# Attention and a depthwise convolution on one core: another order of the first loads and statistics, and q and k projected in pairs ahead of the scores

## The chip, the cores and the metric

The program runs on one core of a Trainium2 chip. The metric is the device time of one execution in microseconds, the median of several. The core has five engines that run their own instruction queues side by side and wait for each other by semaphores: TensorE (PE, matrix products), VectorE (DVE, elementwise work and statistics), ScalarE (ACT, activations and copies), GpSimd (POOL) and SyncE (SP). Transfers are issued from the queues of SyncE, GpSimd and, at the end, ScalarE.

## The reference

Input x has 16 images of 384 channels and 32 by 32 pixels, so 1024 positions. Everything is float32. Two layers follow each other, each added to its input:

```python
# layer 0
g = group_norm(x)                      # 32 groups of 12 channels, over group and positions
q, k, v = g @ w_qkv.T                  # 8 heads of 48 channels
a = softmax(q @ k.T * 48 ** -0.5)      # 1024 x 1024 for each head and image
x = x + (a @ v) @ w_proj.T + b_proj
# layer 1
w = mean of the four 90-degree rotations of the 7 x 7 filters
x = x + depthwise_conv_7x7(group_norm(x), w, pad=3)
```

## The kernel before

**Tiling.** Channels lie on partitions, in three blocks of 128 (`NK = 3`); positions lie along the free dimension. Heads are worked in pairs, a pair being a unit, so an image has four units. A unit is done in two halves of 512 query positions, and a half is a group of eight steps. A step makes the scores of 128 keys against 512 queries for both heads (`s_step`, TensorE, line 472, into one of three PSUM buffers), ScalarE exponentiates them (line 480, into one of eight buffers), and `av_step` (line 488) multiplies them with v and accumulates. TensorE thus alternates: eight score steps, eight steps with v, and so on, 64 of each in an image. After each half ScalarE copies the accumulator out (`take`, line 499).

**Between the groups** TensorE has other work: q and k of the next image (`qk_step`, line 421, twelve 512-column matmul instructions each, copied from PSUM by ScalarE at line 428; q and k of one of three channel blocks are a pair), v at the start of an image (`v_step`, line 447), and the projection of the image before (`proj_step`, line 541). The first and the last image are projected at once, in parts (`proj_part`, line 579).

**The softmax sums** come out of the product with v as an extra row. They go through DRAM to be spread over partitions, are inverted (`invert`, line 513) and multiplied in (`divide`, line 524) on VectorE.

**Group norm of x.** Image 0 has its statistics from VectorE (line 239) and the averages over groups from TensorE with masks (`groups_on_pe`, line 307). Image 1's go through DRAM (`x_channels`, `gather`, `groups`, `spread`). Images 2 to 15 are read a first time for their statistics alone, as 42 pieces of 512 KB (`stream_in` on GpSimd's queue, `stream_stats` on VectorE, line 361, through six buffers). Once all are in, one gather (`stream_gather`), one evaluation (`stream_groups`) and one spread (lines 404 and 410) give the scale and shift of all of them, `x_sc`. When an image is loaded for its projection (`load_x`, line 155, into the one x buffer, once v of the image before has been projected), ScalarE normalises it in place (`x_apply`, line 338, three activations).

**Group norm of the sum x1.** For most images the mean comes from ScalarE's accumulators (`x1_means`, line 943), the squares from three more activations (`x1_squares`, line 270), and scale and shift from ScalarE's Ln and Exp (`x1_groups`, lines 288 to 290, with two table loads) and a spread through DRAM (lines 259 and 263). Then three activations make the normalised xn (`x1_chains`, line 338, output `xn`). For the images in `ON_VECTOR` VectorE makes the statistics instead.

**The convolution** is 49 multiply-and-adds ("taps") for each image and channel block on VectorE (line 607), up to three blocks taken in turn. For the last two images some blocks are done on TensorE instead, as products with diagonal matrices (line 712), added by VectorE (line 727). The last block of all is summed in two halves that line 867 adds. Stores to `out` go from GpSimd's queue (line 620).

**Order.** Nothing is scheduled at run time. The Python program keeps two clocks, `clock` for TensorE and `vclock` for VectorE, and writes each engine's instructions in the order of a planned time. `after(wait, cost, f)` puts work for VectorE (and GpSimd's transfers) at a due time; `catch_up(clock)` writes due work, and taps in what is left. `applies` is the queue of ScalarE's normalisations with due time and cost; `act_slot(free)` writes those that are due and fit into `free` us. `chunks` holds the pairs of q and k to be issued, and `other` decides, twice in a group (after the scores and after the products with v), whether a projection or a piece of `chunks` goes in there. `ready[b]` is the planned time from which image b is normalised. Before, a counter of credit, 0.45 more at each call, let two chunks through when it had reached 2, in whichever of the two places that was:

```python
def other(done):
    credit = min(credit + 0.45, 2.0)
    ...
    elif credit >= 2:
        while chunks and credit >= 1:
            ...
            if kind == "qk" and i % 2 == 0:
                act_slot(4.5)
            issue(chunks.popleft())
            credit -= 1
```

At the end the program checks that no softmax sum is out of range (`check_vector`, `check_tensor`), and would otherwise run a slower general version (`run(True)`), which never happens with these inputs.

Of the kernel before, what the change touches and what calls it, by code (L numbers as in the profile page):

```python
# [44 lines left out]
def kernel(  # L45
# [47 lines left out]
    again = consts.tile([1, 1], I32, name="again")  # L93
    wsym = consts.tile([P, NK, KS, KS], F32, name="wsym")


    with tc.tile_pool(name="wcpool", bufs=1) as wcpool:
        wc = wcpool.tile([P, NK, KS, KS], F32, name="wc")
        nc.gpsimd.dma_start(
            wc.rearrange("p k i j -> p k (i j)"),  # L100
            w_conv.rearrange("(k p) o i j -> p k (o i j)", p=P),
        )
        w90 = wcpool.tile([P, NK, KS, KS], F32, name="w90")
        nc.vector.tensor_tensor(
            w90, wc, wc[:, :, :, ::-1].rearrange("p k a b -> p k b a"), ALU.add
        )
        nc.vector.tensor_tensor(wc, w90, w90[:, :, ::-1, ::-1], ALU.add)
        nc.vector.tensor_scalar(wsym, wc, 0.25, None, ALU.mult)

    def run(general):  # L110
        tag = "g" if general else "f"
        with ExitStack() as stack:
# [37 lines left out]

            def load_x(b):
                xns[b] = xpool.tile([P, NK, N], F32, tag="x", name=f"x_{b}")
                queue = nc.gpsimd if b else nc.sync
                for k in range(NK):
                    queue.dma_start(  # L155
                        xns[b][:, k, :], x[b, k * P : (k + 1) * P].rearrange("p h w -> p (h w)")
                    )
# [662 lines left out]
            def after(wait, cost, f):  # L820

                nonlocal count
                count += 1
                heapq.heappush(later, (now() + wait, count, cost, f))
# [83 lines left out]
            lims = []  # L908

            applies, pending = deque(), []  # L910
            ON_VECTOR = (B - 3, B - 2)

            def project(b):
                nonlocal clock
# [47 lines left out]

            def x1_groups(b, st):
                st.groups_x1()
                applies.append((clock + 8.0, 3.7, lambda: x1_chains(b, st)))

            def act_slot(free):

# [77 lines left out]
            late["masks"] = masks_0.rearrange("p (b c) -> p b c", c=P)  # L1046
            st.groups_on_pe(late["masks"])
            for k in range(NK):
                engine = (nc.vector, nc.gpsimd, None)[k]
                st.apply(xns[0][:, k, :], xns[0][:, k, :], k, engine)  # L1050
            ready[0] = 0.0
            queue(0)
            every = [(b, k) for b in range(2, B) for k in range(NK)]
            for n, bk in enumerate(every):
                after(4.0 * n, 0.0, lambda bk=bk: stream_in(*bk))
                after(4.0 * n + 10.0, 1.3, lambda bk=bk: stream_stats(*bk))
            after(4.0 * len(every) + 14.0, 0.0, stream_gather)
            after(4.0 * len(every) + 34.0, 3.6, stream_groups)

            def check_vector():  # L1060

                lim = small.tile([P, 2], F32, tag="lim", name="lim")
                every = sums.rearrange("p u c -> p (u c)")
                nc.vector.tensor_reduce(lim[:, 0:1], every, AX.X, ALU.max)
                nc.vector.tensor_reduce(lim[:, 1:2], every, AX.X, ALU.min)
                nc.vector.tensor_scalar(lim[:, 0:1], lim[:, 0:1], SUM_HIGH, None, ALU.is_le)
                nc.vector.tensor_scalar(lim[:, 1:2], lim[:, 1:2], SUM_LOW, None, ALU.is_ge)
                ones = small.tile([P, 1], F32, tag="ones", name="ones")
                nc.vector.memset(ones, 1.0)
                lims.append((ones, lim))  # L1070
# [27 lines left out]
                if (h, part) == (1, 1):  # L1098
                    after(6.0, 1.2, lambda: conv_on_pe_end(b, k))

            def other(done):

                nonlocal credit
                credit = min(credit + 0.45, 2.0)
                catch_up(clock)
                if proj and proj[0][0] <= clock:
                    project(proj.popleft()[1])
                elif credit >= 2:
                    while chunks and credit >= 1:
                        kind, cb, i = chunks[0]  # L1110
                        first = {"qk": 2 * NT * (i // 2), "rest": 2 * NT * 3}[kind]
                        if ready.get(cb, 1e9) > clock or done < first:
                            break
                        if kind == "qk" and i % 2 == 0:
                            act_slot(4.5)
                        issue(chunks.popleft())
                        credit -= 1
                catch_up(clock)

            def fast_finish(b):  # L1120
# [24 lines left out]
                    return True  # L1145
                return False

            credit = 0.0
            for b, n0, size in [
                (b, b * PER_B + sum(SIZES[:g]), SIZES[g]) for b in range(B) for g in range(len(SIZES))  # L1150
            ]:
                r = n0 - b * PER_B
                if n0 == NS - PER_B:
                    last_image = clock
                if r == 0:
                    while chunks:
                        issue(chunks.popleft())
                    if b + 1 < B:
                        queue(b + 1)
                for n in range(n0, n0 + size):  # L1160
                    s_step(n)
                clock += (size * US_STEP + US_TURN) / 2
                if r == 0 and b - 1 == FAST[0]:
                    fast_end(b - 1)
                if r == 0:
                    for i in range(NT // 2):
                        issue(("v", b, i))
                ending = b in FAST and r + size == PER_B
                if ending:
                    catch_up(clock)  # L1170
                    divide_at_once(NP * b + NP - 1, 0)
                    vclock += 4.2
                    for o in range(NK):
                        proj_part(b, o, (0, 1))
                    clock += 2 * US_PROJ
                else:
                    if r and pending and b - 1 in FAST:
                        applies.append((clock, 3.7, pending.pop()))
                    catch_up(clock)
                    act_slot(4.5)  # L1180
                    other(r + size)
                for n in range(n0, n0 + size):
                    av_step(n)
                    u, h, i = n // (2 * NT), n // NT % 2, n % NT
                    if i == NT - 1:
                        take(u, h)
                clock += (size * US_STEP + US_TURN) / 2
                if n0 // (2 * NT) < (n0 + size) // (2 * NT):
                    finish((n0 + size) // (2 * NT) - 1)
                if ending:  # L1190
                    catch_up(clock)
                    assert not invs and not waiting
                    fast_finish(b)
                else:
                    other(r + size)
                if b == 1 and r == 0:
                    conv_prepare()
                    nc.sync.dma_start(wp, w_packed)
                if b == B - 1:

                    if once("mat_0", r >= 16):
                        mat = flat2(xpool.tile([P, NK, N], F32, tag="x", name="mat_0"))
                        conv_matrices(0, mat)
                        late["w3"] = mat[:, 2 * SH * KS * CH :][:, 0:C]
                    if once("w", r >= 32 and b - 1 in x1_stats):
                        nc.sync.dma_start(wp, w4[:, 0:NK])
                        nc.sync.dma_start(late["w3"], w4[:, NK])
                    if once("mat_1", r >= 24):
# [12 lines left out]
                if b == B - 1 and r in (32, 40, 48):  # L1221
                    loads(1)
# [3 lines left out]
            fast_end(B - 1)  # L1226
            clock += 7.0
            vclock = clock
            after(4.0, 2.6, check_vector)
            while later or chains or active or pe_conv:  # L1230
                if pe_conv:
                    if pe_conv[0][0] == B - 1 and lims:
# [53 lines left out]
```

## Time and profile before

| | us |
|---|---|
| time, median of 3 (2974.22 to 2976.72) | 2974.3 |
| span of the profiled execution | 2976.5 |
| TensorE busy | 2926.9 (98%) |
| VectorE busy | 2580.1 (87%) |
| ScalarE busy | 1414.6 (48%) |
| GpSimd busy | 198.7 (7%) |

In the profile a line such as `L421 PE MATMUL ps_qk<-x,wqk` names the source line, the engine, the operation, and what it writes and reads. In the timeline the first two numbers are the start and the length of a run of like instructions in us, `x24` is how many they are, and the bracket says how long the engine had been idle before and who released it. Many numbers overlap, since the engines run side by side; idle time counts only where it is TensorE's, or whatever engine sets the end.

### The profile page before, as it was taken

How to read it: one execution, taken by the hardware profiler on the slowest of the kernel's cores; microseconds unless marked ns; L12 is line 12 of the kernel's file. 1: busy time of each engine (PE TensorE's matmuls, PEld its weight loads, DVE VectorE, ACT ScalarE, POOL GpSimd, SP SyncE). 2: the span in 40 equal slices, each digit the busy share in tenths (PEclk: the TensorE clock that was granted, in tenths of full speed). 3: DMA queues.
4: the chain of work that ended last, by engine and by line, in shares of the span. 5: the costliest groups of instructions: out<-in, count | busy, mean ns of one | idle time of the engine just before them, and what ended most of it. 6: DMA issues, size and time to landing. Idle time of an engine off the chain costs nothing.

```text
span 2976.5 us, 30347 instructions
## 1 busy us (share of the span) xinstructions
PE 2926.9 (98%) x11590; PEld 1185.5 (40%) x11590; DVE 2580.1 (87%) x2596; ACT 1414.6 (48%) x1683; POOL 198.7 (7%) x307
## 2 busy tenths in 40 slices
PE   7999899999999999999999999999999999999997
PEld 4334343343434434343343434334343433434333
DVE  0535990999989999899998999899998999999998
ACT  2432445445464544645545464555436464444610
POOL 0311201000000100000000000000000000000000
PEclk9999999999999999999999999999999999999999
DMA  2741112031311203121121312202131220312324
GB/s 74 254 116 41 24 31 72 15 67 37 69 34 33 68 24 66 37 62 41 26 70 30 66 37 56 47 22 60 44 66 37 46 57 15 67 37 52 108 57 115
DMA packets 72460, 169.72 MB, mean 57 GB/s; under 512 B 30080, under 2 KB 32496, under 8 KB 70768
## 3 DMA queue, kind: packets, MB, share of 16 engines
q0 software_dynamic: 29760, 97.67, 12.1%
q1 hardware_dynamic: 40784, 66.40, 9.8%
q10 hardware_dynamic: 1760, 3.61, 0.5%
q8 instruction: 93, 1.52, 0.2%
q14 instruction: 63, 0.52, 0.1%
HBM read 120.18 MB, written 29.35 MB: 50 GB/s over the span
## 4 chain that ended last, share of the span: by engine, by line


## 5 line engine op out<-in xcount | busy, mean ns | idle before, releaser
L607 DVE SCALAR_TENSOR_TENSOR x<-xn,wsym,x 128x899 f32<-128x899 f32 (+11 forms) x2181 | 2351.0, 1149 | 29.7 <-ACT xn L338 29.7
L480 ACT ACTIVATE e<-ps_s 128x1024 f32<-128x1024 f32 x1024 | 952.4, 1051 | 54.6 <-PE ps_s L472 51.4
L472 PE MATMUL ps_s<-qk 48*128 48x512 f32 x4096 | 914.2, 596 | 0.0
L488 PE MATMUL acc<-e,v 128*64 128x512 f32 x4096 | 907.2, 595 | 0.0
L472 PEld LDWEIGHTS ps_s<-qk 48*128 48x128 f32 x4096 | 376.8, 185 | 533.7 <-ACT e L480 257.2
L421 PE MATMUL ps_qk<-x,wqk 128*128 128x512 f32 x1152 | 512.6, 602 | 18.1 <-ACT x L338 15.8
L488 PEld LDWEIGHTS acc<-e,v 128*64 128x64 f32 x4096 | 283.2, 137 | 607.9 <-issue 601.7
L499 ACT COPY o<-acc 128x512 f32<-128x512 f32 x128 | 75.2, 587 | 644.9 <-PE acc L488 644.9
L421 PEld LDWEIGHTS ps_qk<-x,wqk 128*128 128x128 f32 x1152 | 217.5, 192 | 310.8 <-issue 275.8
L428 ACT COPY qk<-ps_qk 128x1024 f32<-128x1024 f32 x96 | 97.2, 1012 | 384.1 <-PE ps_qk L421 384.1
L447 PE MATMUL ps_v<-wv,x 128*128 128x384 f32 x768 | 254.7, 492 | 0.0
L541 PE MATMUL ps_proj<-o,wp 128*128 128x512 f32 x504 | 218.6, 592 | 0.0
L447 PEld LDWEIGHTS ps_v<-wv,x 128*128 128x128 f32 x768 | 146.0, 192 | 110.3 <-ACT e L480 11.4
L524 DVE TENSOR_TENSOR o<-o,inv 128x1024 f32<-128x1024 f32 x62 | 75.4, 1217 | 132.1 <-DMA inv<-inv 110.9
L456 ACT COPY v<-ps_v 128x384 f32<-128x384 f32 x128 | 55.1, 483 | 187.1 <-PE ps_v L447 187.1
L541 PEld LDWEIGHTS ps_proj<-o,wp 128*128 128x128 f32 x504 | 95.8, 190 | 117.6 <-issue 111.9
L155 POOL DMA_DIRECT2D x<-in_x x45 | 24.1, 543 | 1503.8 <-PE ps_v L447 1308.1
L361 DVE BATCH_NORM_STATS2 bs_all<-xs 128x6 f32<-128x512 f32 x84 | 52.1, 679 | 82.7 <-DMA xs<-in_x 82.7
L549 ACT ACTIVATE x<-ps_proj,bp 128x1024 f32<-128x1024 f32 x42 | 46.8, 1115 | 126.4 <-PE ps_proj L541 126.4
L712 PE MATMUL ps_conv<-sh,mat 128*32 128x464 f32 (+3 forms) x784 | 83.9, 584 | 0.0
L338 ACT ACTIVATE xn<-x,sc_x 128x1024 f32<-128x1024 f32 x44 | 52.1, 1284 | 28.6 <-DVE sc_x L328 28.5
L338 ACT ACTIVATE x<-x,x_sc 128x1024 f32<-128x1024 f32 x42 | 48.9, 1229 | 17.4 <-DMA x_sc<-gr_all 17.4
(110 smaller groups left out, 536.5 us busy)
## 6 DMA issues: line engine op xcount, KB each, us to landing
x<-in_x POOLq DMA_DIRECT2D x93, 512.0 KB, 5.4
inv<-inv SPq DMA_DIRECT2D x124, 256.0 KB
out<-x POOLq DMA_DIRECT2D x48, 512.0 KB, 3.6
xs<-in_x POOLq DMA_DIRECT2D x42, 512.0 KB, 6.0
qk<-qk SPq DMA_DIRECT2D x96, 128.0 KB
sh<-xd SPq DMA_DIRECT2D x34, 160.0 KB
o<-o SPq DMA_DIRECT2D x84, 64.0 KB
sh<-xd ACTq DMA_DIRECT2D x22, 160.0 KB
```

Source lines behind the costliest of these rows:

```text
L338: nc.scalar.activation(dst, src, AF.Identity, bias=self.sc[:, k, 1:2], scale=self.sc[:, k, 0:1],)
L421: nc.tensor.matmul(ps[:, h, :], lhsT=wqk[:, k, s, t, :], rhs=xns[b][:, k, h * HALF : (h + 1) * HALF], start=(k == 0), stop=(k == NK - 1),)
L428: nc.scalar.copy(halves(qks[u][:, s, :]), ps)
L447: nc.tensor.matmul(ps[:, j, 0:C], lhsT=xns[b][:, k, t * P : (t + 1) * P], rhs=wv[:, k, :], start=(k == 0), stop=(k == NK - 1),)
L472: nc.tensor.matmul(ps[:, j, :], lhsT=qks[u][r, 1, i * P : (i + 1) * P], rhs=qks[u][r, 0, h * HALF : (h + 1) * HALF], start=True, stop=True,)
L480: nc.scalar.activation(es[n], ps, AF.Exp, scale=SCALE)
L488: nc.tensor.matmul(accs[u, h][64 * j : 64 * j + 64, :], lhsT=v_of(u, i, j), rhs=e[:, j, :], start=(i == 0), stop=(i == NT - 1),)
L499: nc.scalar.copy(os_[u][:, h * HALF : (h + 1) * HALF], accs.pop((u, h)))
L524: nc.vector.tensor_tensor(os_[u], os_[u], invs.pop(u), ALU.mult)
L541: nc.tensor.matmul(ps[:, h, :], lhsT=wp[:, t, o * P : (o + 1) * P], rhs=os_[NP * b + t][:, h * HALF : (h + 1) * HALF], start=(t == 0), sto ...
L607: nc.vector.scalar_tensor_tensor(acc, xn1s[b, k].rearrange("p (h w) -> p h w", w=W)[:, iy, ix], wsym[:, k, dy + PAD, dx + PAD : dx + PAD + 1],
L712: nc.tensor.matmul(pss[b, k][CH * i : CH * (i + 1), h, :].rearrange("p (y x) -> p y x", x=W)[:, :, ox], lhsT=mats[k][:, i, d0 * KS + dx + ...
```

## The change

The change has five parts.

1. The weights of the convolution keep buffers of their own (`wc` in `consts`), and VectorE symmetrises them (`conv_weights`) after image 0's statistics and normalisation, not before. Image 0's three blocks are normalised by VectorE, ScalarE and VectorE, not VectorE, GpSimd and ScalarE.
2. Image 1 is loaded from SyncE's queue, not GpSimd's, and the 42 statistics pieces are planned every 3 us, not every 4.
3. q and k are projected only after the products with v, ahead of the next scores, always as a pair, and up to 9 us of ScalarE's normalisations go in front of the pair's copies. The credit goes.
4. `ON_VECTOR` loses image 13, whose second statistics now come from ScalarE; the xn normalisations are due 6.5 us, not 8, after `x1_groups`.
5. Of the range check three quarters are done early (`check_early`), and the rest at the end.

The aim is to start TensorE earlier, to have the statistics early, and to keep ScalarE's work inside pieces in which TensorE has something else to do.

```diff
-    with tc.tile_pool(name="wcpool", bufs=1) as wcpool:
-        wc = wcpool.tile([P, NK, KS, KS], F32, name="wc")
...
-        nc.vector.tensor_tensor(wc, w90, w90[:, :, ::-1, ::-1], ALU.add)
+    wc = consts.tile([P, NK, KS, KS], F32, name="wc")
...
+    def conv_weights():
+        nc.vector.tensor_tensor(
+            wsym, wc, wc[:, :, :, ::-1].rearrange("p k a b -> p k b a"), ALU.add
         )
+        nc.vector.tensor_tensor(wc, wsym, wsym[:, :, ::-1, ::-1], ALU.add)
         nc.vector.tensor_scalar(wsym, wc, 0.25, None, ALU.mult)
...
-                queue = nc.gpsimd if b else nc.sync
+                queue = nc.gpsimd if b > 1 else nc.sync
...
-            ON_VECTOR = (B - 3, B - 2)
+            ON_VECTOR = (B - 2,)
...
-                applies.append((clock + 8.0, 3.7, lambda: x1_chains(b, st)))
+                applies.append((clock + 6.5, 3.7, lambda: x1_chains(b, st)))
...
-                engine = (nc.vector, nc.gpsimd, None)[k]
+                engine = (nc.vector, None, nc.vector)[k]
                 st.apply(xns[0][:, k, :], xns[0][:, k, :], k, engine)
+            conv_weights()
...
-                after(4.0 * n, 0.0, lambda bk=bk: stream_in(*bk))
-                after(4.0 * n + 10.0, 1.3, lambda bk=bk: stream_stats(*bk))
-            after(4.0 * len(every) + 14.0, 0.0, stream_gather)
-            after(4.0 * len(every) + 34.0, 3.6, stream_groups)
+                after(3.0 * n, 0.0, lambda bk=bk: stream_in(*bk))
+                after(3.0 * n + 10.0, 1.4, lambda bk=bk: stream_stats(*bk))
+            after(3.0 * len(every) + 14.0, 0.0, stream_gather)
+            after(3.0 * len(every) + 34.0, 3.6, stream_groups)
+            EARLY = NP * (B - 4)
+            def check_early():
+                for key, op in (("max", ALU.max), ("min", ALU.min)):
+                    many[key] = wpool.tile([P, 2], F32, name=f"sums_{key}")
+                    nc.vector.tensor_reduce(many[key][:, 0:1], sums[:, 0:EARLY, :], AX.XY, op)
...
-                nc.vector.tensor_reduce(lim[:, 0:1], every, AX.X, ALU.max)
-                nc.vector.tensor_reduce(lim[:, 1:2], every, AX.X, ALU.min)
+                nc.vector.tensor_reduce(many["max"][:, 1:2], sums[:, EARLY:, :], AX.XY, ALU.max)
+                nc.vector.tensor_reduce(many["min"][:, 1:2], sums[:, EARLY:, :], AX.XY, ALU.min)
+                nc.vector.tensor_reduce(lim[:, 0:1], many["max"], AX.X, ALU.max)
+                nc.vector.tensor_reduce(lim[:, 1:2], many["min"], AX.X, ALU.min)
...
-            def other(done):
-                nonlocal credit
-                credit = min(credit + 0.45, 2.0)
+            def other(done, scores_next):
                 catch_up(clock)
                 if proj and proj[0][0] <= clock:
                     project(proj.popleft()[1])
-                elif credit >= 2:
-                    while chunks and credit >= 1:
...
-                        if kind == "qk" and i % 2 == 0:
-                            act_slot(4.5)
+                elif scores_next and chunks:
+                    kind, cb, i = chunks[0]
+                    first = {"qk": 2 * NT * (i // 2), "rest": 2 * NT * 3}[kind]
+                    if ready.get(cb, 1e9) <= clock and done >= first:
+                        act_slot(9.0)
                         issue(chunks.popleft())
-                        credit -= 1
+                        if kind == "qk":
+                            issue(chunks.popleft())
...
-                    other(r + size)
+                    other(r + size, False)
...
-                    other(r + size)
+                    other(r + size, True)
+                if b == B - 4 and r == 32:
+                    after(0.0, 2.0, check_early)
...
-            after(4.0, 2.6, check_vector)
+            after(4.0, 1.2, check_vector)
```

More of the change, by code (lines that the diff above doesn't have):

```diff
@@ L94 @@
     wsym = consts.tile([P, NK, KS, KS], F32, name="wsym")
-    with tc.tile_pool(name="wcpool", bufs=1) as wcpool:
-        wc = wcpool.tile([P, NK, KS, KS], F32, name="wc")
-        nc.gpsimd.dma_start(
-            wc.rearrange("p k i j -> p k (i j)"),
-            w_conv.rearrange("(k p) o i j -> p k (o i j)", p=P),
-        )
[L103 to L106, printed above, removed]
-        nc.vector.tensor_tensor(wc, w90, w90[:, :, ::-1, ::-1], ALU.add)
+    wc = consts.tile([P, NK, KS, KS], F32, name="wc")
+    nc.gpsimd.dma_start(
+        wc.rearrange("p k i j -> p k (i j)"),
+        w_conv.rearrange("(k p) o i j -> p k (o i j)", p=P),
+    )
+    def conv_weights():
+        nc.vector.tensor_tensor(
+            wsym, wc, wc[:, :, :, ::-1].rearrange("p k a b -> p k b a"), ALU.add
+        )
+        nc.vector.tensor_tensor(wc, wsym, wsym[:, :, ::-1, ::-1], ALU.add)
         nc.vector.tensor_scalar(wsym, wc, 0.25, None, ALU.mult)
@@ L1054, in run @@
             for n, bk in enumerate(every):
-                after(4.0 * n, 0.0, lambda bk=bk: stream_in(*bk))
-                after(4.0 * n + 10.0, 1.3, lambda bk=bk: stream_stats(*bk))
-            after(4.0 * len(every) + 14.0, 0.0, stream_gather)
-            after(4.0 * len(every) + 34.0, 3.6, stream_groups)
+                after(3.0 * n, 0.0, lambda bk=bk: stream_in(*bk))
[7 more added lines that the diff above has]
+                    nc.vector.tensor_reduce(many[key][:, 0:1], sums[:, 0:EARLY, :], AX.XY, op)
             def check_vector():
                 lim = small.tile([P, 2], F32, tag="lim", name="lim")
-                every = sums.rearrange("p u c -> p (u c)")
-                nc.vector.tensor_reduce(lim[:, 0:1], every, AX.X, ALU.max)
-                nc.vector.tensor_reduce(lim[:, 1:2], every, AX.X, ALU.min)
+                nc.vector.tensor_reduce(many["max"][:, 1:2], sums[:, EARLY:, :], AX.XY, ALU.max)
+                nc.vector.tensor_reduce(many["min"][:, 1:2], sums[:, EARLY:, :], AX.XY, ALU.min)
+                nc.vector.tensor_reduce(lim[:, 0:1], many["max"], AX.X, ALU.max)
+                nc.vector.tensor_reduce(lim[:, 1:2], many["min"], AX.X, ALU.min)
                 nc.vector.tensor_scalar(lim[:, 0:1], lim[:, 0:1], SUM_HIGH, None, ALU.is_le)
@@ L1107, in other @@
                     project(proj.popleft()[1])
-                elif credit >= 2:
-                    while chunks and credit >= 1:
[L1110 to L1113, printed above, removed]
-                        if kind == "qk" and i % 2 == 0:
-                            act_slot(4.5)
+                elif scores_next and chunks:
[3 more added lines that the diff above has]
+                        act_slot(9.0)
                         issue(chunks.popleft())
-                        credit -= 1
+                        if kind == "qk":
+                            issue(chunks.popleft())
                 catch_up(clock)
@@ L1146, in once @@
                 return False
-            credit = 0.0
             for b, n0, size in [
```

## The prediction

> **What bounds the kernel now.** I read the busy time by stages first, then TensorE's own timeline for its idle stretches, then who ended them, then the first 22 us and the last 20.
>
> Stages (columns: length, busy us of TensorE, of its weight loads, of VectorE, ScalarE, GpSimd, then granted clock, DMA share, GB/s):
>
> ```profile
> 22.00:330.00 308.00, 291.56 (x1032) 122.10 (x1034) 137.42 (x197) 117.08 (x136) 65.59 (x104) 0.96 0.36 106
> 330.00:2450.00 2120.00, 2120.00 (x8079) 853.93 (x8076) 1932.94 (x1841) 1098.68 (x1318) 102.72 (x156) 1.00 0.20 47
> 2450.00:2860.00 410.00, 410.00 (x1616) 161.79 (x1615) 403.03 (x430) 195.33 (x228) 17.07 (x26) 1.00 0.22 54
> 2860.00:2977.00 117.00, 98.96 (x840) 41.51 (x838) 100.16 (x113) 1.32 (x2) 6.94 (x8) 0.91 0.37 100
> ```
>
> From 330 to 2860 us TensorE is busy for all of the 2530 us at full clock, and its matmuls follow each other at one fixed step (429 ns per 512-column pair). Nothing can be won there by moving work: only at the two ends. VectorE has 187 us of slack in the long stage, so it does not set the end there.
>
> TensorE's idle stretches after its start, and their makers:
>
> ```profile
> 120.80 7.09 PE L488 MATMUL acc<-e,v 128*64 128x512 f32 x32
> 130.47 11.98 PE L421 MATMUL ps_qk<-x,wqk 128*128 128x512 f32 x24 [2.59 <-ACT x L338]
> 286.83 7.09 PE L488 MATMUL acc<-e,v 128*64 128x512 f32 x32
> 302.29 3.27 POOL L410 DMA_DIRECT2D x_sc<-gr_all  x3 [20.71 <-issue]
> 305.83 3.51 ACT L338 ACTIVATE x<-x,x_sc 128x1024 f32<-128x1024 f32 x3 [17.36 <-DMA x_sc<-gr_all]
> 307.12 12.40 PE L421 MATMUL ps_qk<-x,wqk 128*128 128x512 f32 x24 [13.20 <-ACT x L338]
> ```
>
> Two stalls. q of image 1 waits 2.59 us for its normalised x; q of image 2 waits 13.20 us, because ScalarE sat 17.36 us on the scale table of images 2 to 15, which GpSimd issued only at 302. And both pieces after a stall are long: 11.98 and 12.40 us against the 10.5 us of an undisturbed one (10.57 at 996), so 1.5 and 1.9 us more.
>
> The head:
>
> ```profile
> 7.55 0.42 DVE L104 TENSOR_TENSOR w<-wc 128x147 f32<-128x147 f32 x1 [7.55 <-DMA wc<-in_w_conv]
> 7.58 1.28 ACT L338 ACT_TABLE_LOAD   x1 [7.58 <-DMA x<-in_x]
> 8.50 3.65 DVE L239 BATCH_NORM_STATS2 bs_x<-x 128x6 f32<-128x512 f32 x6
> 21.93 33.94 PE L421 MATMUL ps_qk<-x,wqk 128*128 128x512 f32 x72 [2.34 <-DVE x L334]
> ```
>
> VectorE waits for the convolution weights, works on them, and only then begins image 0's statistics, though the third and last piece of x was there at 7.58.
>
> ScalarE in the middle, where the change moves its normalisations, and the tail:
>
> ```profile
> 1001.54 1.01 ACT L428 COPY qk<-ps_qk 128x1024 f32<-128x1024 f32 x1 [1.35 <-PE ps_qk L421]
> 1018.36 0.29 ACT L290 ACTIVATE af_x<-mv_x,af_x 32x1 f32<-32x1 f32 x1
> 1020.79 0.59 ACT L499 COPY o<-acc 128x512 f32<-128x512 f32 x1 [2.14 <-PE acc L488]
> 1029.10 3.55 ACT L338 ACTIVATE xn<-x,sc_x 128x1024 f32<-128x1024 f32 x3
> ```
>
> ```profile
> 2954.70 5.92 PE L712 MATMUL ps_conv<-sh,mat 128*32 128x464 f32 x52
> 2962.54 1.23 DVE L867 TENSOR_TENSOR x<-x,sum 128x1024 f32<-128x1024 f32 x1
> 2963.68 1.22 DVE L727 TENSOR_TENSOR x<-ps_conv,x 128x1024 f32<-128x1024 f32 x1
> 2965.19 0.53 POOL L620 DMA_DIRECT2D out<-x  x1 [0.60 <-DVE x L727]
> ```
>
> TensorE's last matmul ends at 2960.62 and VectorE's last addition, which needs it, starts 3.06 us later, since VectorE still has taps of its own. From the last store's issue to the end of the span it is 11.3 us.
>
> **What the Trainium skill says.** "TensorE: Matmul & The Clock Gate", What's actually happening: after an idle window of about 3.4 us the array runs at half clock until it has been busy for as long. The trace agrees: the weight loads of the first pieces stand 0.85 us apart until 27.8 us and 0.43 after, and a 12.40 us piece follows the 13.20 us stall. So a stall removed gives back its clock loss too. "DMA: Bandwidth & Descriptors", Two DMAs through the same engine are not ordered: descriptors of one queue start in order; so weight loads queued on SyncE right behind image 0 should not delay it. No run here shows that yet. "PSUM — Partial Sum Buffer", Engine vs sequencer instructions: ScalarE's queue is strict FIFO; the trace agrees, the accumulator copy at 309.24 stood behind the waiting normalisation.
>
> **The change part by part.**
> 1. Convolution weights go behind image 0's statistics. Three operations (0.42 + 0.31 + 0.24) and the wait until 7.55 leave the head. The last piece's two statistics (3.65/3 = 1.2 us) can start at 7.58 and end at 8.8, against 12.15: 3.3 us, if the first two pieces landed 1.2 and 2.4 us before the third, as three equal loads on one queue should. If all three land together it is 7.58 + 3.65 = 11.23: 0.9 us. I take 3.3. The weights (wqk), which waited for the freed memory until 8.61, now go out early; they are needed at 18.6. VectorE and ScalarE instead of GpSimd normalise k = 1, 2: nothing, since the matmuls of k = 0 (3.4 us at half clock) hide both.
> 2. Image 1 is loaded from SyncE, so the loads for statistics of images 2 to 15 no longer stand behind it on GpSimd until 81 us; 22 of 42 run while TensorE projects image 0. VectorE has the 19 that stand ahead of image 1 done when image 1 arrives at about 83 (79.3 − 3.3 + 7), where before it was still at them until 104. Its scale should be there at about 110, its normalisation stands at 119. Stall 2.59 + 1.5 = 4.1 us gone.
> 3. The table for images 2 to 15: with loads every 3 us and an early start, the last statistics come at about 150 (before 194), held by VectorE's in-order waits for unit 0's and 1's sums. Gather and regroup some 20 us, groups after unit 2's sums at 171, 20 us for the 8-byte spread (20.71 in the row above), 7 more: ready at about 210, needed at 270. Stall 13.20 + 1.9 = 15.1 us gone.
> 4. q and k as pairs between products with v and scores. In the built order there are 45 such pairs outside image 0 before and after, each with the same neighbours' switch (about 0.09 us), so 0.0 us for TensorE. The risk is ScalarE: in one piece per image stand three squares (4.1 us), as half the images had before with no stall (996 to 1002). In the next stand image b's three xn normalisations, which waited a whole group longer before. Scale and shift leave ScalarE at 1018.65; GpSimd's second DMA is issued 4.2 to 4.5 us later where no output store stands ahead of it (5.3 to 7.0 where one does; in the built order none does now) and lands in 2.3 to 4.1, median 2.6. So: scale at 1025.6, normalised 1029.2, q's copy done 1030.2. TensorE needs that buffer for its second score step at 1020.67 + 10.5 + 0.9 = 1032.1. Slack 1.9 us, and 0 with the slowest landing. I take 0.
> 5. Image 13's statistics go to ScalarE: six bn_stats (4.1 us) and a dozen small operations leave VectorE; x1 chains begin earlier. 11 fewer taps stand after the last normalisation in the built order (36, not 47), about 10 us. The check's two reductions (1.21 each over 1024 columns) run over a quarter, about 0.35 each plus two of 0.14: 1.4 us. Together VectorE comes 11 us earlier, but only the 3.06 us up to TensorE's end count. With the last store alone on its queue I add 0.2: 3.3 us.
>
> Sum: 3.3 + 4.1 + 15.1 + 0.0 + 3.3 = 25.8; 2974.3 − 25.8 = 2948.5.
>
> **The rivals.**
> - A, the new piece waits: the scale lands later by DMA traffic and each of 13 images loses about 1 us of TensorE: 2948.5 + 13 = 2961.5. For it: slack is under 2 us. Against: the store ahead of it is gone.
> - B, image 2 still stalls, the table being late by another wait (VectorE held on sums, or the spread slower beside loads): 2948.5 + 15.1 = 2963.6. Against: 60 us of slack.
> - C, the tail or the head gives nothing, VectorE or the loads being slower: 2952 to 2954.
> - D, slower: both DMAs of the spread at their slowest in every image (6.4 for 3.7, 4.1 for 2.6: 4.2 us late) hold q's copy to 1034.4; the exponentials then trail the scores and 2.8 us a piece are lost, 13 times: 36 us, 2985. For it only single slowest landings.
>
> **How the numbers follow.** Forecast 0.60, C 0.14, A 0.13, B 0.09, D 0.04. The range takes the forecast, C and the nearer part of A and B: low 2943 is the forecast with 5 us from shorter landings at the end and a shorter cold start; high 2963. Faster by over 0.2% (under 2968.4): all but D and a mix of A and B, 0.93; same 0.04; slower 0.03.
>
> **What would show it.** First q matmul at 18.6 us; no TensorE gap over 0.3 us between there and the last image; GpSimd's table DMA near 200; q pieces of 10.5 us everywhere; the last addition right after TensorE's last matmul. Wrong if gaps of 1 us recur behind the pieces with xn normalisations, or if q of image 2 still waits on ScalarE.

## The result, and the profile after

| | before | after |
|---|---|---|
| time, median of 6 runs of each, taken by turns | 2974.69 us | 2951.72 us |
| lowest to highest | 2974.22 to 2976.72 | 2950.06 to 2953.00 |
| span of the profiled execution | 2976.5 us | 2950.1 us |
| TensorE, VectorE, ScalarE busy | 2926.9, 2580.1, 1414.6 us | 2921.9, 2576.3, 1421.5 us |

The ratio is 0.9921, interval 0.9909 to 0.9934: faster by 23.0 us. The ranges in this document leave out two executions, one of e4_spacing of 3848.91 us at a granted clock of 0.75 and one of e10_best of 12180.91 us at 1.00. Hardly any work has gone, as the busy times show. In the two traces TensorE idles 21.4 us less, at both ends, and is 5.0 us less busy with the same products, part of which ran at a lower clock before.

The stages of the kernel after, in the columns of the prediction (length, busy us of TensorE, its weight loads, VectorE, ScalarE, GpSimd, granted clock, DMA share, GB/s):

```profile
22.00:330.00 308.00, 307.03 (x1103) 127.82 (x1104) 161.93 (x218) 125.75 (x145) 63.84 (x94) 0.99 0.34 103
330.00:2450.00 2120.00, 2120.00 (x8071) 853.28 (x8068) 1943.08 (x1853) 1093.32 (x1312) 102.50 (x156) 1.00 0.19 47
```

In the first 330 us TensorE is now idle for 1.0 us, where it was for 16.4, at a clock of 0.99 and not 0.96. The long stage is full, as it was.

The head, from the timeline:

```profile
7.88 1.29 DVE L239 BATCH_NORM_STATS2 bs_x<-x 128x6 f32<-128x512 f32 x2 [0.84 <-DMA x<-in_x]
19.00 3.78 PE L421 MATMUL ps_qk<-x,wqk 128*128 128x512 f32 x4 [2.38 <-DVE x L334]
19.59 0.41 DVE L104 TENSOR_TENSOR wsym<-wc 128x147 f32<-128x147 f32 x1
```

VectorE now waits for nothing but x. Its last two statistics start when the third piece lands, at 7.88, and the weights of the convolution are worked on at 19.59, when TensorE already runs. The first product with w_qkv starts at 19.00 instead of 21.93.

Image 2, which had stood for 13.20 us, from the timelines of GpSimd, ScalarE and TensorE:

```profile
196.74 3.27 POOL L410 DMA_DIRECT2D x_sc<-gr_all  x3 [19.92 <-DMA gr_all<-af_all]
281.90 3.55 ACT L338 ACTIVATE x<-x,x_sc 128x1024 f32<-128x1024 f32 x3
280.44 7.09 PE L488 MATMUL acc<-e,v 128*64 128x512 f32 x32
287.46 10.57 PE L421 MATMUL ps_qk<-x,wqk 128*128 128x512 f32 x24
```

GpSimd issues the table at 197, not at 302; ScalarE's line has no bracket, so it waited for nothing; and TensorE goes from the products with v straight into q of image 2, which takes 10.57 us and not 12.40. Image 1, which had stood for 2.59 us, goes the same way, from the timelines of ScalarE and TensorE:

```profile
119.22 3.56 ACT L338 ACTIVATE x<-x,sc_x 128x1024 f32<-128x1024 f32 x3
138.88 10.57 PE L421 MATMUL ps_qk<-x,wqk 128*128 128x512 f32 x24
```

The middle, where three normalisations now stand inside a piece of q and k (ScalarE, and TensorE's piece around it):

```profile
996.84 0.29 ACT L290 ACTIVATE af_x<-mv_x,af_x 32x1 f32<-32x1 f32 x1
999.28 0.58 ACT L499 COPY o<-acc 128x512 f32<-128x512 f32 x1 [2.14 <-PE acc L488]
1003.75 3.50 ACT L338 ACTIVATE xn<-x,sc_x 128x1024 f32<-128x1024 f32 x3 [3.88 <-DMA sc_x<-gr_x]
1007.15 0.99 ACT L428 COPY qk<-ps_qk 128x1024 f32<-128x1024 f32 x1
```

```profile
999.16 10.57 PE L421 MATMUL ps_qk<-x,wqk 128*128 128x512 f32 x24
1009.66 7.14 PE L472 MATMUL ps_s<-qk 48*128 48x512 f32 x32
```

ScalarE does stand still for its scale, 3.88 us here and 55.0 us over 13 images in the list of waits, and q's copy stands behind it. The copy is done at 1008.1 all the same; counted as in the prediction, TensorE needs that buffer at 999.2 + 10.5 + 0.9 = 1010.6, so 2.5 us were left, and the scores follow without a bracket. A wait on an engine with room is not a cost until it reaches the engine that has none.

The tail:

```profile
2924.58 13.32 PE L712 MATMUL ps_conv<-sh,mat 128*32 128x464 f32 x124
2928.15 1.23 DVE L867 TENSOR_TENSOR x<-x,sum 128x1024 f32<-128x1024 f32 x1
2938.01 1.23 DVE L727 TENSOR_TENSOR x<-ps_conv,x 128x1024 f32<-128x1024 f32 x1 [8.63 <-PE ps_conv L712]
2939.53 0.53 POOL L620 DMA_DIRECT2D out<-x  x1 [9.33 <-DVE x L727]
```

Before, VectorE came 3.06 us after TensorE's last product. Now it has been waiting for it for 8.63 us. The two ends have changed places by 11.7 us.

Where the gain arises is seen by comparing the start of the same instruction in both traces, stage by stage. TensorE's order of images is the same, so each difference is the gain up to that point:

| up to | before, us | after, us | gained since the row above |
|---|---|---|---|
| v of image 0 | 62.86 | 59.56 | 3.30 |
| first scores of image 1 | 242.44 | 235.55 | 3.59 |
| first product after v of image 1 | 272.48 | 266.15 | -0.56 |
| v of image 2 | 432.04 | 410.53 | 15.18 |
| v of image 15 | 2711.28 | 2689.43 | 0.34 |
| end of TensorE | 2960.62 | 2937.91 | 0.86 |
| end of the span | 2976.50 | 2950.13 | 3.66 |

Sum 26.4 us. The median gained 23.0. The difference lies in the execution of before that was profiled: it took 2978.29 us by its own device time, 3.6 us over the median, and the one of after 2951.93, 0.2 over.

### The profile page after: what moved, and what is told of

Read it like the earlier page. It is cut to its first block, busy times and chain, and to the rows that moved or that the text cites. A ratio compares the mean times of both kernels' runs of the same rounds, so it can differ in the third digit from the quotient of the medians.

```text
span 2950.1 us, 30344 instructions
## 1 busy us (share of the span) xinstructions
PE 2921.9 (99%) x11590; PEld 1189.3 (40%) x11590; DVE 2576.3 (87%) x2582; ACT 1421.5 (48%) x1694; POOL 198.9 (7%) x303
## 4 chain that ended last, share of the span: by engine, by line
PE 86%; DVE 6%; issue 6%; DMA 1%; POOL 0%; ACT 0%; SPq 0%; POOLq 0%; DVEq 0%; ACTq 0%
PE ps_s L472 27%; PE acc L488 27%; PE ps_qk L421 16%; PE ps_v L447 8%; PE ps_proj L541 6%; DVE x L607 5%; PE ps_conv L712 1%; PE ps_proj L579 1%; DVE sum L607 0%; DMA x<-in_x 0%; PE ps_st_x L307 0%; DMA inv<-inv 0%; DMA sh<-xd 0%; DVE bs_x L239 0%; DVE o L524 0%
## 5 line engine op out<-in xcount | busy, mean ns | idle before, releaser
L155 POOL DMA_DIRECT2D x<-in_x x42 | 22.4, 542 | 1631.5 <-PE ps_v L447 1485.9
L712 PE MATMUL ps_conv<-sh,mat 128*32 128x496 f32 (+3 forms) x784 | 83.2, 580 | 1.7 <-DMA sh<-xd 1.7
L556 POOL DMA_DIRECT2D x<-in_x x42 | 36.6, 871 | 311.4 <-ACT x L549 302.0
```

What stands on the lines that cost most here:

```text
L712: nc.tensor.matmul(pss[b, k][CH * i : CH * (i + 1), h, :].rearrange("p (y x) -> p y x", x=W)[:, :, ox], lhsT=mats[k][:, i, d0 * KS + dx + ...
```

## The experiments

My theory: the gain is the two removed stalls, the earlier head and a VectorE that is out of the way at the end. The rival: the new rule for q and k, with ScalarE's work inside the pieces, is what pays; and a second, that TensorE's gain at the start is the gain at the end, whatever VectorE does. Some runs put one part, or a pair of parts, into the kernel before, others take one part out of the changed kernel, and the last try what the trace still leaves open. Not taken apart are the two edits of the head and the three for the end (image 13's statistics, 6.5 us for 8, the early check).

**The rule for q and k taken back, in the changed kernel (e1_credit).**

```diff
-            def other(done, scores_next):
+            def other(done):
+                credit = min(credit + 0.45, 2.0)
...
-                elif scores_next and chunks:
+                elif credit >= 2:
+                    while chunks and credit >= 1:
...
-                        act_slot(9.0)
+                        if kind == "qk" and i % 2 == 0:
+                            act_slot(4.5)
```

> The changed kernel with the old rule for q and k (credit, either place between groups, 4.5 us of normalisations ahead of a pair); all else as changed. Mine: TensorE was already full in the middle, and the two rules give it the same number of pieces, so 2951.7 as the changed kernel, within 1.5 us; images 3 to 14 take 175.3 us each as in both kernels. VectorE has about 7 us more of taps after the last normalisation, which the 8.6 us that it waits for TensorE at the end of the changed kernel just hold. Rival (ScalarE's work inside the pieces is what gains): at least a third of the 23 us is lost, 2959 or more, with gaps of TensorE in the middle.

Measured: 2949.79 us (2949.63 to 2950.51, 5 runs), ratio 0.9917 [0.9904, 0.9931], against the changed kernel's 0.9921. The intervals lie over each other: the rule by itself brings no gain that can be measured here (the changed kernel is, if anything, 1.9 us slower than this run), and the images between take 175.3 us each with it and without. The rival falls.

**The head alone, in the kernel before (e5_head).**

```diff
+    wc = consts.tile([P, NK, KS, KS], F32, name="wc")
...
+    def conv_weights():
...
-                engine = (nc.vector, nc.gpsimd, None)[k]
+                engine = (nc.vector, None, nc.vector)[k]
...
+            conv_weights()
```

> The kernel before with only the head's edits: the convolution's weights behind image 0's statistics, and VectorE, ScalarE, VectorE for its three blocks. Mine: the first q matmul comes 3 us earlier and everything behind moves with it, the stalls of images 1 and 2 included, since what they wait for moves too: 2974.7 - 3 = 2971.7. Rival (the stalls absorb it, their transfers being timed by the loads): 2974.7.

Measured: 2972.15 us (2970.12 to 2976.18, 19 runs), ratio 0.9989 [0.9982, 0.9996]. TensorE starts at 18.93, 3.0 us earlier, and the gain survives although both stalls are still there (2.31 us at 124, 12.21 us at 287). They move along, because what they wait for starts earlier too: GpSimd issues image 2's table at 294.4, and in e6_end below, which has the old head, at 298.0.

**Image 1 from SyncE alone (e3_queue), 3 us spacing alone (e4_spacing), and both (e2_stream), in the kernel before.**

```diff
-                queue = nc.gpsimd if b else nc.sync
+                queue = nc.gpsimd if b > 1 else nc.sync
```

```diff
-                after(4.0 * n, 0.0, lambda bk=bk: stream_in(*bk))
+                after(3.0 * n, 0.0, lambda bk=bk: stream_in(*bk))
```

> The kernel before with only image 1's load on SyncE. The loads for statistics start at about 21 us in place of 81, but their evaluation stays where it was planned, behind image 0's last normalisation on VectorE, and GpSimd's power for it behind the load of image 2. Mine: the stall of image 1 goes (4.1 us), that of image 2 stays at 13 to 15: 2970.4. Rival (an early start of the loads is enough): 2955.

Measured: 2971.60 us (2970.15 to 2973.62, 12 runs), ratio 0.9987 [0.9979, 0.9996]. Image 1's stall is gone, and image 2's stands. TensorE's timeline:

```profile
300.64 4.64 PE L421 MATMUL ps_qk<-x,wqk 128*128 128x512 f32 x5 [11.59 <-ACT x L338]
```

> The kernel before with only the 3 us spacing. The evaluation now stands on VectorE ahead of image 0's last division, but the loads still start at 81 us behind image 1's load. Mine: image 2's stall goes, but image 1's statistics stand behind 19 pieces and not 14 (6 us later), and VectorE holds image 0's last division until the table's gather is there, so TensorE stalls near 205 to 225 by 5 to 15 us: together with 7 us more of taps at the end 2972, between 2965 and 2982. Rival (the spacing alone is the gain): 2959 or less.

Measured: 2980.90 us (2978.09 to 2984.42), ratio 1.0018 [1.0009, 1.0028]: slower than before. Image 2 no longer waits, but image 1's normalisation now holds TensorE up for longer, and earlier than I had thought. Timelines of VectorE, ScalarE and TensorE:

```profile
87.77 24.37 DVE L361 BATCH_NORM_STATS2 bs_all<-xs 128x6 f32<-128x512 f32 x38 [66.07 <-DMA xs<-in_x]
112.05 3.65 DVE L239 BATCH_NORM_STATS2 bs_x<-x 128x6 f32<-128x512 f32 x6
```

```profile
135.54 3.50 ACT L338 ACTIVATE x<-x,sc_x 128x1024 f32<-128x1024 f32 x3 [13.87 <-DMA sc_x<-gr_x]
```

```profile
140.48 7.14 PE L472 MATMUL ps_s<-qk 48*128 48x512 f32 x20 [10.55 <-ACT e L480]
```

VectorE first needs all the 19 pieces that the denser plan puts ahead of image 1, and with image 1 still in front of them on GpSimd's queue they only arrive from 87 us on. So image 1's statistics start at 112. The plan now has image 1's normalisation ahead of an exponential, ScalarE sits on it, and TensorE stops inside image 0's scores. The order of the plan is only worth something if the data arrive in that order.

> The kernel before with two edits: image 1 loaded from SyncE and the statistics pieces every 3 us. Mine: both early stalls go, 4.1 + 15.1 = 19.2 us off TensorE, and q of image 2 starts near 288 and not at 307; but VectorE's taps then do not start earlier by as much, 9 more of them stand after the last normalisation (about 7.4 us), and the end, which hung on VectorE by 3.06 us before, hangs on it by some 10: 2974.5 - 19.2 + 7.4 = 2962.7. Rival (VectorE's tail follows TensorE): 2955.3. Rival (the table is still late): 2970 or more.

Measured: 2969.63 us (2964.98 to 2971.86, 17 runs), ratio 0.9983 [0.9976, 0.9990]. In the trace TensorE has all of its gain: v of image 2 starts 20.9 us earlier than in the trace of before, and its last product ends at 2940.30, 20.3 us earlier. But the span is only 13.3 us shorter. The end of its timeline says why:

```profile
2937.63 2.67 PE L712 MATMUL ps_conv<-sh,mat 128*32 128x496 f32 x20
2949.03 1.21 DVE L727 TENSOR_TENSOR x<-ps_conv,x 128x1024 f32<-128x1024 f32 x1
2951.27 1.23 DVE L867 TENSOR_TENSOR x<-x,sum 128x1024 f32<-128x1024 f32 x1
2952.80 0.53 POOL L620 DMA_DIRECT2D out<-x  x1 [1.73 <-DVE x L867]
```

TensorE is done at 2940.3 and VectorE is still on its taps until 2951.3, without a bracket at its lines: it is the bound. It has 79 taps left after its last normalisation, 79.3 us, where the kernel before had 70, 71.9 us. The second rival falls: of TensorE's 20.3 us some 7 are lost to VectorE's tail. By the medians the gain is smaller still, 5.3 us. The profiled execution, 2964.98 us, is the fastest of the 17, 4.7 us under their median, and that of before is 3.4 us over the median of the runs beside it; why executions of this kernel differ that much is not known.

**The end alone, in the kernel before (e6_end).**

```diff
-            ON_VECTOR = (B - 3, B - 2)
+            ON_VECTOR = (B - 2,)
...
-                applies.append((clock + 8.0, 3.7, lambda: x1_chains(b, st)))
+                applies.append((clock + 6.5, 3.7, lambda: x1_chains(b, st)))
...
+            def check_early():
...
-            after(4.0, 2.6, check_vector)
+            after(4.0, 1.2, check_vector)
```

> The kernel before with only the edits for the end: image 13 off ON_VECTOR, 6.5 us for 8, three quarters of the range check early. Mine: two taps fewer and 1.4 us less of check behind the last normalisation are 3.2 us, of which the 3.06 count that VectorE ended behind TensorE: 2971.6. Rival (VectorE is not what ends the span): 2974.7.

Measured: 2971.05 us (2969.32 to 2975.69, 13 runs), ratio 0.9985 [0.9976, 0.9993]. The timeline:

```profile
2949.45 6.13 PE L712 MATMUL ps_conv<-sh,mat 128*32 128x464 f32 x54
2955.77 1.22 DVE L727 TENSOR_TENSOR x<-ps_conv,x 128x1024 f32<-128x1024 f32 x1
```

TensorE ends at 2955.58 and VectorE's addition follows 0.2 us later, not 3.06, still without a wait: 68 taps are left after its last normalisation and not 70.

**The changed kernel without the end edits (e9_noend)**, the same diff the other way round.

> The changed kernel without the edits for the end (ON_VECTOR, 8 us and the whole check as before). Mine: TensorE ends as in the changed kernel, but 17 more taps (14.6 us) and 1.4 us of check stand on VectorE behind the last normalisation, against the 8.6 us that it had to spare: about 7.5 us after TensorE's last matmul, 2959. Rival (VectorE follows TensorE, the edits for the end are worth their 3 us): 2954.7 or less.

Measured: 2961.07 us (2959.05 to 2961.60, 5 runs), ratio 0.9945 [0.9931, 0.9958]. The timeline:

```profile
2943.42 1.08 DVE L607 SCALAR_TENSOR_TENSOR x<-xn,wsym,x 128x841 f32<-128x841 f32 x1
2944.54 1.23 DVE L867 TENSOR_TENSOR x<-x,sum 128x1024 f32<-128x1024 f32 x1
2945.68 1.22 DVE L727 TENSOR_TENSOR x<-ps_conv,x 128x1024 f32<-128x1024 f32 x1
```

TensorE ends at 2937.37, within 0.6 us of the changed kernel, but VectorE comes 8.3 us after it, not 3.06. By the times of the two profiled executions the end edits are worth 2959.97 - 2951.93 = 8.0 us inside the change. There they leave VectorE 59 taps after its last normalisation and not 76; in the kernel before, the same edits took off only 2, and TensorE's end left them 3.06 us to win. Why the order that the program writes gives 17 taps in one case and 2 in the other was not traced. So the parts do not add: the loads alone gave 5.3 us, the head 2.7 and the end 3.8, by the medians beside them, 11.8 together, and the change gave 23.0.

**What is left (e11_changed, e7_rows, e8_halves, e10_best).** The changed kernel has one new idle stretch, in TensorE's timeline of the convolution:

```profile
2863.28 4.09 PE L712 MATMUL ps_conv<-sh,mat 128*32 128x496 f32 x32
2869.08 3.49 PE L712 MATMUL ps_conv<-sh,mat 128*32 128x512 f32 x31 [1.70 <-DMA sh<-xd]
```

It waits for shifted rows of image 14, whose load SyncE issues at 2862.2, right behind the stores of the last image's rows at 2861.3. In e7_rows that load is written ahead of them:

```diff
             conv_piece()
+            loads(1)
             fast_end(B - 1)
```

e8_halves adds and stores the last block in two halves on top of it, e10_best has both and the old rule for q and k, and e11_changed is the changed kernel once more beside them.

> The changed kernel once more, as the measure for the runs beside it: 2951.7.

> The changed kernel with image 14's next shifted rows asked for before the last image's stores and not behind them. Mine: TensorE ends the span and idled 1.70 us on these rows at 2867, so 1.7 us: 2950.0. Rival (the rows then delay the stores, and TensorE waits later for the same time): 2951.7.

> As e7_rows, and the last block is added and stored in two halves, the first while TensorE still works on the second. Mine: behind TensorE's end stand an addition of 512 and not 1024 columns (0.67 for 1.23 us) and half the bytes (about 0.6 us): 2948.8. Rival (the end is the fixed part of the store): 2949.5 or more.

> The kernel of e1_credit (the old rule for q and k) with both edits of e8_halves. Mine: TensorE ends 1.2 us earlier than with pairs, as in e1_credit, but it idled only 0.61 us on the rows there; 2949.8 - 0.6 - 1.2 = 2948.0, if VectorE's 7 us more of taps still end before TensorE. Rival (VectorE then ends the span): 2949.8 or more.

Measured: e11_changed 2950.60 us (2949.29 to 2953.36, 5 runs), 0.9919 [0.9906, 0.9933]. e7_rows 2948.17 (2947.59 to 2948.85, 4 runs), 0.9908 [0.9893, 0.9923]: the fastest here, 2.4 us under e11_changed, with no run in common between the two ranges, though the intervals of the ratios overlap. Its timeline:

```profile
2927.89 1.23 DVE L867 TENSOR_TENSOR x<-x,sum 128x1024 f32<-128x1024 f32 x1
2933.24 1.22 DVE L727 TENSOR_TENSOR x<-ps_conv,x 128x1024 f32<-128x1024 f32 x1 [4.12 <-PE ps_conv L712]
```

The gap is gone (it was 0.90 us in the trace of e11_changed), and the gain is larger than the 1.7 us forecast. TensorE ends at 2933.08, 2.3 us before that of e11_changed, and VectorE still has 4.12 us to spare. A part of this is TensorE's clock, as the last section shows.

e8_halves: 2948.48 (2947.55 to 2951.15, 4 runs), 0.9910 [0.9895, 0.9925]: no gain over e7_rows. In the trace the stretch from TensorE's end to the end of the span is indeed shorter, 11.1 us for 12.7, but the two halves share a PSUM tile, and TensorE now waits for VectorE's first half addition (line 732):

```profile
2929.15 0.69 DVE L732 TENSOR_TENSOR x<-ps_conv,x 128x512 f32<-128x512 f32 x1
2929.90 5.82 PE L712 MATMUL ps_conv<-sh,mat 128*32 128x464 f32 x56 [0.90 <-DVE x L732]
```

e10_best: 2950.41 (2949.98 to 2950.86), 0.9915 [0.9900, 0.9930], slower than e7_rows by 2.2 us. Here TensorE ends at 2934.28 and VectorE last:

```profile
2936.16 1.23 DVE L877 TENSOR_TENSOR x<-x,sum 128x1024 f32<-128x1024 f32 x1
2937.30 0.68 DVE L732 TENSOR_TENSOR x<-ps_conv,x 128x512 f32<-128x512 f32 x1
```

Its last addition comes 3.0 us after TensorE, as the rival of its forecast had it. With the old rule VectorE finishes the other sum of the last block (line 867 of the other kernels) 8.3 us later than in e7_rows. So the rule for q and k does have a use: VectorE gets there 6.5 us (e1_credit against the changed kernel) to 8.3 us earlier, which the changed kernel, with 8.63 us to spare there, does not need, and one with a shorter convolution does.

The execution of e10_best that took 12180.91 us stays open. It is four times as long, at a granted clock of 1.00, and has no trace. A fast version followed by the general one, as the program runs them when a softmax sum is out of range, could look like this, but that is not shown. For this kernel, then, that the general version never runs with these inputs is not certain.

## Why the prediction was right

1. **The head.** Forecast 3.3, measured 2.93 at the first q product (19.00, forecast 18.6, before 21.93) and 2.7 by the median of e5_head. That it is 3.30 by v of image 0 is luck: q and k of image 0 took 33.56 us in this execution and 33.94 in that of before. The assumption behind it, that the pieces of x land one after another, held: VectorE had done the first two, four operations from 4.47 to 7.04, before the third landed. What the prediction concluded from the Trainium skill's "DMA: Bandwidth & Descriptors", Two DMAs through the same engine are not ordered, and could not see, that weight loads behind x on one queue do not delay it, holds within 0.3 us (third piece at 7.88, before 7.58).
2. **Image 1.** Forecast 4.1, measured 3.59, and 0.56 of it lost again behind image 1's first scores, where 0.33 us of waiting appeared. The normalisation starts at 119.22, forecast 119, and e3_queue shows that the queue does this. (Before, VectorE was at the pieces ahead of image 1 until 107.2, and these were 14; the prediction has 104, on which no term rests.) But 1.5 of the 4.1 us, the longer piece behind the stall, is no fixed price: e5_head and e6_end have stalls of 2.31 and 2.84 us here, and the piece behind takes 10.57 us in both.
3. **Image 2.** Forecast 15.1, measured 15.18 between v of image 1 and v of image 2. The table came at 197 to 200, forecast near 200. The queue alone leaves this stall (11.59 us in e3_queue). The spacing alone removes it (e4_spacing), but pays with 10.55 us in image 0's scores; only both together give the gain.
4. **The pieces.** Forecast 0.0, measured 0.34 over 13 images. The slack of 1.9 us held against a wait that was really there. Rivals A and D, in which it reaches TensorE, did not occur: TensorE has no gap over 0.3 us between image 2 and the convolution.
5. **The end.** Forecast 3.3, measured 3.66 after TensorE's end; VectorE relative to TensorE moved by 11.7 us, forecast 11. As the price of the part, though, 3.3 is too small: e9_noend shows 8.0. The step subtracted 3.06 us of before, and took for granted that VectorE would otherwise keep up with a TensorE 22 us earlier; without these edits it would not have. The forecast's sum holds only because VectorE's 11 us cover this too, which is luck as far as the reasoning goes.

The measured 2951.72 us lies 3.2 above the forecast and next to rival C's 2952. It is the traces that decide against C: head and tail both gave what they should, and rival B's stall is gone.

The sum of 25.8 us matched the two traces, 26.4, better than the two medians, 23.0. The forecast set a median of 2974.3 against stalls read off one execution of 2978.29 us; counted from that execution it would have been 2952.5. e6_end has the same start as before, and its profiled execution (2970.75 us) is one at its median. In it TensorE reaches v of image 2 at 427.71, 4.3 us earlier than the 432.04 of before. Nearly all of this lies in few places: q of image 1 takes 10.57 us and not 11.98, the products of one column and v of image 1 give 1.7 us, the start up to v of image 0 0.6, and the two stalls together 0.6 (2.84 for 2.59, 12.32 for 13.20). So most of it is TensorE's clock. Behind image 1's stall the windows of before and of e6_end show, in this order (columns as above):

```profile
130.00:134.00 4.00, 3.53 (x5) 1.64 (x6) 1.29 (x2) 3.16 (x4) 0.39 (x2) 0.58 0.93 288
```

```profile
130.00:134.00 4.00, 3.86 (x9) 1.82 (x10) 1.29 (x2) 2.82 (x4) 0.53 (x1) 1.00 1.01 303
```

The granted clock is 0.58 in one and 1.00 in the other. The prediction charged every stall with a loss of clock, though the 2.59 us of image 1 are shorter than the idle window of 3.4 us that it went by. The four stalls of 11.59 to 13.20 us on q of image 2 (before, e3_queue, e5_head, e6_end) agree: the piece behind takes 12.37 to 13.16 us in all of them. After the stalls of 2.31 to 2.84 us it came in one trace of three. A second trace of before was not taken, and what decides in which execution the clock falls after a short stall stays open.

Not foreseen: the wait of 1.70 us for shifted rows, which e7_rows removes, and the lower clock in v of image 1, which no part of the change touches.

## What to carry to other kernels

Take the time from which you subtract from the same execution as the stalls, and look at a second execution before you price what comes behind a short stall. When the engine that bounds a kernel is to be made earlier, ask whether the one that ends it can follow: here 20 us won on TensorE shortened the traced span by 13 until VectorE's tail was cut too. An order planned for the data is only as good as the queue that brings them: change the two together, since one alone gave little here and the other alone made the kernel slower.

## What the runs showed of the hardware

TensorE's clock fell without any long idle stretch in the profile. When v of image 1 begins, behind 28 products of one column each (line 307) between which TensorE is idle for 0.64 us at most, the clock is down. The kernel after shows:

```profile
243.21 1.72 PE L307 MATMUL ps_st_x<-mn_x,masks 128*128 128x1 f32 x14
245.57 3.05 PE L307 MATMUL ps_st_x<-d_x,masks 128*128 128x1 f32 x14 [0.64 <-DVE d_x L322]
248.48 17.73 PE L447 MATMUL ps_v<-wv,x 128*128 128x384 f32 x48
```

and in windows over these stretches (columns as above):

```profile
244.00:249.00 5.00, 4.36 (x24) 4.24 (x24) 0.64 (x4) 0.70 (x1) 0.03 (x1) 0.67 0.02 5
249.00:253.00 4.00, 4.00 (x8) 2.09 (x7) 2.07 (x3) 1.24 (x1) 2.56 (x2) 0.56 0.00 0
253.00:257.00 4.00, 4.00 (x13) 2.30 (x13) 4.00 (x5) 0.86 (x2) 0.00 (x0) 1.00 0.00 0
```

The granted clock is 0.67, then 0.56, and then 1.00; the 48 products take 17.73 us, and those of image 2, at full clock, 15.75. The Trainium skill's "TensorE: Matmul & The Clock Gate", What's actually happening, speaks of an idle window of about 3.4 us; here a stretch of very short products, in which the profile counts TensorE as busy for 4.36 of 5 us, was enough. It cost 2.0 us, and 2.8 in the kernel before (18.50 us). In each of the 13 traces of this case the clock is at 0.50 to 0.67 in the first 3 us of this v, which takes 17.1 to 18.6 us.

Behind the same 28 products ahead of the last image's convolution it happens in 11 of the 13 traces, and not in those of e7_rows and e9_noend. The windows of the kernel after and of e7_rows show, in this order:

```profile
2859.00:2864.00 5.00, 5.00 (x37) 1.48 (x40) 3.83 (x6) 1.24 (x1) 3.17 (x2) 0.66 0.47 158
```

```profile
2859.00:2864.00 5.00, 5.00 (x52) 1.57 (x50) 3.95 (x6) 1.24 (x1) 2.62 (x2) 1.00 0.30 117
```

37 products in 5 us at a clock of 0.66, 52 at 1.00. What decides it was not tried. What it is worth depends on what comes next, as e9_noend shows, which has the full clock but not e7_rows' edit:

```profile
2859.53 6.67 PE L712 MATMUL ps_conv<-sh,mat 128*32 128x464 f32 x60
2868.72 22.21 PE L712 MATMUL ps_conv<-sh,mat 128*32 128x512 f32 x216 [2.52 <-DMA sh<-xd]
```

Its 60 products take 6.67 us and not 8.37 as in the kernel after, and then TensorE waits 2.52 us for the shifted rows and not 1.70: the rows set the time. With the rows there in time the clock counts. From the end of the one-column products to its own end TensorE takes 78.9 us in the kernel after, 78.3 in e11_changed and 77.8 in e9_noend; with the edit it takes 75.9 in e10_best, where the clock is 0.67 in the same window of 5 us, and 74.2 in e7_rows. So the edit shortens this stretch at either clock, and some 1.6 us of e7_rows' earlier end is the clock.
